# Kept one-hot stores and loads moved from the SyncE queue to the ScalarE queue

## The chip, the cores and the metric

One core of a Trainium2 chip runs the whole program. Its engines are TensorE (PE in the profile, with PEld for the weight loads that overlap it), VectorE (DVE), ScalarE (ACT), GpSimd (POOL) and SyncE (SP). Each engine runs its own instructions in order and waits for other engines at semaphores. A DMA is an instruction of the engine that issues it; the transfer itself runs on 16 DMA engines. The metric is the device time of one execution in microseconds, lower is better.

## What is computed

A block with three parts, on 16 batches of a 32x512 tensor: a point-cloud graph network (the "xattn" part), a Mamba-style scan layer, and a gated feed-forward layer. The change lies in the first part, and there in the gathering of neighbours:

```python
inds_sorted = _sorted_indices(coords.transpose(0, 2, 1))   # 4 space-filling-curve orders of 512 nodes
inds_list = [_window_inds(s) for s in inds_sorted]         # windows of k = 10 neighbours in each order
...
def _get_graph_features(feats, inds_list, perm, W_lin, b_lin, k=K):
    center = feats[:, :, None, :]
    for inds in inds_list:
        neigh = gather(feats, inds)
        gf = concatenate([broadcast(center), neigh - center], axis=-1)
    ...
    scores = einsum('bihd,bjhd->bhij', qh, qh) / sqrt(headdim)
    attn = softmax(scores, axis=-1)
    out = einsum('bhij,bjhd->bihd', attn, qh)
    fused = out @ W_lin.T + b_lin
...
g1 = _get_graph_features(f0, inds_list, perm1, W_lin1, b_lin1)       # layer 1
h1 = einsum('oc,bnkc->bonk', W_conv1, g1);  feats1 = max_k(lrelu(instance_norm(h1)))
g2 = _get_graph_features(feats1, inds_list, perm2, W_lin2, b_lin2)   # layer 2, the same orders
```

Both layers use the same four orders, so they gather through the same permutations.

## The kernel before

All of the graph part is in `graph_part`, in an order written out by hand (L384 switches the planner off). The 16 batches are four groups of four (NBG = 4), and each group has two layers. The eight pairs of group and layer are run as blocks in the order of L1024: (0,0), (1,0), (0,1), (2,0), (1,1), (3,0), (2,1), (3,1). A block has NGRP = 43 iterations of 12 nodes each, and the main loop (L1070) runs through all 344 of them as a software pipeline. In one iteration it emits, in this order: `expo` of the iteration before (a matmul L868 on PE and an exponential L873 on ACT), `turn` (DVE), `scores` (PE, L844 and L851), `rest` and `reduce` (DVE), perhaps one `rank_step` (PE L540, ACT L541), `greatest` (DVE L860), `mapped` (PE L913, ACT copy L918), `sums` (DVE L880), `steps` (see below), `shares` (DVE L886, POOL L888), perhaps another `rank_step`, `outputs` (PE L941), and `differences` for the iteration six ahead (POOL L809). After every third `differences` four DMAs follow (L819, DX<-DD), which SP issues once POOL is done.

`steps` advances a generator, `prep` (L627), by one or two yields. It prepares the next block: every node's position in each order (`rank`) is turned into one-hot matrices `oh` (DVE L751, two orders to a tile of 128x2x512 bf16, 256 KB), and `place` (L701) sorts the features by matmuls with them into `pp` (PE L705, 12 matmuls for a pair of tiles). ACT copies `pp` to `so` (L712), and SP stores it (L716, dS), loads the centres (L681, crep) and loads the sorted features back in windows' layout (L725, fs).

For groups 1 and 2 (`KEPT`, L623) the one-hots made for layer 0 are kept: `keep_it` (L757) stores each tile in DRAM as soon as DVE has written it. That makes 64 stores, k<-oh, 32 in block (0,0) and 32 in block (0,1). In layer 1 of these groups (`at_hand`) they are loaded again instead of being made: `prep` puts the pair (tile, source) in the list `transfers` (L747), and the end of the loop body (L1104) issues what is in the list, after `differences`. That makes 64 loads, oh<-k, 32 in block (2,0) and 32 in block (3,0). There are four `oh` buffers, two pairs; in the `at_hand` form a pair of tiles is loaded in one step of `prep`, and the pair loaded two pairs before is placed in the step ahead of it, which frees its buffers. For the first eight iterations of such a block `steps` takes two steps in an iteration, and then one (L1059 with PREP = 42).

Every DMA of the kernel is issued by SP, in the order in which the code emits it. SP waits for the semaphores of one DMA before it goes on to the next.

Of the kernel before, what the change touches and what calls it, by code (L numbers as in the profile page):

```python
# [53 lines left out]
def kernel(ctx: ExitStack, tc: tile.TileContext, I, out):  # L54
# [65 lines left out]
    with ExitStack() as cx:  # L120
        graph_part(nc, tc, cx, I, dram, id32, ones, xt, U, layernorm_steps, rstd_steps, scan_input)
# [256 lines left out]
def graph_part(nc, tc, cx, I, dram, id32, ones, xt, F0, layernorm_steps, rstd_steps, scan_input):  # L378
# [83 lines left out]
    for t, reps, f in (  # L462
# [4 lines left out]
            out=t4, in_=t4, compare_op=ALU.not_equal, fill=f, base=0,  # L467
            pattern=[[0, reps], [-1, NB], [0, K]], channel_multiplier=1,
        )
    for t, n, f in ((mL.rearrange("p i q -> p (i q)"), P, 1.0), (mR, NI * QB, -BIG)):  # L470
        nc.gpsimd.affine_select(
            out=t, in_=t, compare_op=ALU.not_equal, fill=f, base=-NB,
# [74 lines left out]
    def ranks_of(b):  # L547

        return FIRST // 2 + HALF * (b + 1) if b < 4 else 4 * M * (b + 1)

    def rank_step(tile_of):

        n = ranked[0]
        if n == 4 * M * B:
            return
        ranked[0] += 1
        if n < FIRST:
            half, k = divmod(n, HALF)
            b, c, m = half % 4, k // 2, 2 * (half // 4) + k % 2
        else:  # L560
            b, k = divmod(n, 4 * M)
            c, m = divmod(k, M)
        if n == 0:
            load_keys(0, (0, 1))
        compare(tile_of(n), b, c, m)
        if n < FIRST:
            if k == 1 and half != 3 and half < 7:
                load_keys((half + 1) % 4, (0, 1) if half < 3 else (2, 3))
        elif k == 4 and b + 1 < B:
            load_keys(b + 1, range(M))  # L570
# [54 lines left out]
    transfers = []  # L625

    def prep(g, layer, early=False):  # L627
# [61 lines left out]
        def tick():  # L689
            for t in list(later):  # L690
                t[0] -= 1
                if t[0] <= 0:
                    later.remove(t)
                    t[1]()
# [6 lines left out]
        def place():  # L701
            b, c, ohs, pp = pend.pop(0)
            for m in range(M):
                for k in range(3):
                    nc.tensor.matmul(  # L705
                        pp[32 * m:32 * m + 32, :], lhsT=F3[k][:, c, 32 * b:32 * b + 32], rhs=ohs[m // 2][:, m % 2],
                        start=(c == 0 and k == 0), stop=(c == 3 and k == 2),
                    )
            if c < 3:
                return  # L710
            so = wk.tile([P, D], F32, tag="so", name=f"so{key}_{b}", bufs=2)
            nc.scalar.copy(so, pp)  # L712
            dS = dram.tile([P, D], F32, name=f"dS{key}_{b}")

            def store():
                nc.sync.dma_start(out=dS, in_=so)  # L716

                if not early:
                    centre(b)
                later.append([3, spread])  # L720

            def spread():
                for m in range(M):
                    r = 32 * b + 8 * m
                    nc.sync.dma_start(  # L725
                        out=fs[r:r + 8, :, :D], in_=dS[32 * m:32 * m + 32].rearrange("(h c) n -> c h n", h=4)
                    )

            later.append([2, store])

        for b in range(4):
            while ranked[0] < ranks_of(4 * g + b):
                yield False
            pp = None
            for c in range(4):
                if c == 0:
                    pp = ps_1.tile([P, D], F32, tag="pp", name=f"pp{key}_{b}")
                if at_hand and len(pend) == 2:
                    place()
                    tick()  # L740
                    yield
                ohs = [
                    wk.tile([P, 2, D], BF16, tag="oh", name=f"oh{key}_{b}_{c}_{i}", bufs=4) for i in range(2)
                ]
                for i, oh in enumerate(ohs):
                    if at_hand:
                        transfers.append((oh, kept[g, b, c, i]))  # L747
                        continue
                    for j in range(2):
                        m = 2 * i + j  # L750
                        nc.vector.tensor_scalar(  # L751
                            oh[:, j], it2, rank[:, c, m, 4 * g + b:4 * g + b + 1], None, ALU.is_equal
                        )
                    if layer == 0 and g in KEPT:
                        kept[g, b, c, i] = dram.tile([P, 2, D], BF16, name=f"k{key}_{b}_{c}_{i}")

                        def keep_it(to=kept[g, b, c, i], oh=oh):  # L757
                            nc.sync.dma_start(out=to, in_=oh)

                        later.append([1, keep_it])  # L760
                    if i == 0:
                        tick()
                        yield
                if pend and not at_hand:
                    place()
                pend.append((b, c, ohs, pp))
                tick()
                yield
# [56 lines left out]
    def begin(at):  # L825
        g, layer = order[at]
        L, co, npair, WA, WC, HB = layers[layer]
        key = keys[at]
        per = 4 // npair
        nst = -(-NGRP // per)  # L830
        mxo = wk.tile([P, npair, D], F32, tag="mxo", name=f"mxo{key}")
        stats = wk.tile([P, npair, nst, 6], F32, tag="stats", name=f"stats{key}")
        state[at] = key, co, npair, WA, made[key][2], per, mxo, stats
# [172 lines left out]
    def junk(q):  # L1006
        return wk.tile([P, D], F32, tag="h3", name=f"usq{q}", bufs=1)
# [35 lines left out]
    def steps(at, gi):  # L1043


        if tails:
            if next(tails[0], tails) is tails:
                tails.pop(0)
            if at + 1 >= len(order) or not at_hand(at + 1):
                return  # L1050
        if at + 1 >= len(order):
            return
        if at + 1 not in ahead:
            if at > 0 and gi < 4 and not at_hand(at + 1):
                return
            g, layer = order[at + 1]
            ahead[at + 1] = [prep(g, layer), PREP[layer + at_hand(at + 1)]]
        a = ahead[at + 1]
        for _ in range(2 if a[1] > NGRP - LEAD - SPARE - gi else 1):  # L1059
            if next(a[0], None) is False:  # L1060
                break
            a[1] -= 1

    def wanted(at):

        return ranks_of(4 * min(NBG, 1 + sum(layer == 0 for _, layer in order[:at + 1])) - 1)
# [3 lines left out]
    for it in range(len(blocks) + 5):  # L1070

        def do(step, lag):
            if 0 <= it - lag < len(blocks):
                step(*blocks[it - lag])

        at, gi = blocks[it] if it < len(blocks) else (len(order), 0)
        if gi == 0 and it < len(blocks):
            begin(at)
        do(expo, 1)
        do(turn, 3)  # L1080
        do(scores, 0)
        do(rest, 5)
        do(reduce, 4)
        if ranked[0] < wanted(at):
            rank_step(later_tile)
        do(greatest, 0)
        do(mapped, 0)
        do(sums, 1)
        if at + 1 == len(order) and gi == 4:
            tails.extend(scan_input(sm, junk(q), q) for q in range(NBG - 1))  # L1090
        steps(at, gi)
        do(shares, 1)
        if ranked[0] < wanted(at) and (at == 0 or gi % 2):
            rank_step(later_tile)
        do(outputs, 3)
        if at == 0 and gi < 8:
            rank_step(later_tile)
        if it + LEAD < len(blocks):
            to, g2 = blocks[it + LEAD]
            if g2 == 0:  # L1100
                for _ in ahead[to][0]:
                    pass
            differences(to, g2)
        for oh, of in transfers:  # L1104
            nc.sync.dma_start(out=oh, in_=of)
        transfers.clear()
    for t in (*tails, scan_input(sm, junk(NBG - 1), NBG - 1)):
        for _ in t:
            pass
# [381 lines left out]
```

## Time and profile before

| | |
|---|---|
| time before, median of 3 runs | 2413.45 us (2412.68 to 2421.74) |
| profiled execution, its own time | 2415.22 us |
| its span, first to last instruction | 2413.5 us |
| PE busy over the span | 2189.1 us, 91% |
| DVE, ACT, POOL busy | 1659.9, 1095.5, 831.8 us |
| graph part | to about 1360 us; scan and feed-forward after it |
| stores k<-oh | 64, issued from 132.0 to 520.1 us |
| loads oh<-k | 64, issued from 581.6 to 1003.9 us |
| duration of one such DMA on SP, min / median / max | 319 / 377 / 2276 ns (stores), 319 / 384 / 1921 ns (loads) |

The profile gives busy time of each engine, idle time with the event that ended it, and the order of instructions on each engine. "SPq" rows are DMA instructions on SP's queue; their duration is the issue, not the transfer. A row such as "PE pp L705 <- DMA oh<-k" means that PE's matmul at L705 stood idle until that transfer had landed. The median and the profiled execution differ by 1.8 us, less than a tenth of a per cent.

### The profile page before, as it was taken

What the parts mean: (1) busy time and instruction counts of PE and PEld (TensorE: products, weight loads), DVE (VectorE), ACT (ScalarE), POOL (GpSimd) and SP (SyncE); (2) the same over time, 40 slices, a digit from 0 to 9 for tenths busy, and PEclk for the clock granted to TensorE, in tenths of its full rate; (3) what the DMA queues carried; (4) which work ended last, traced back from release to release, by engine and by line L of the source; (5) the groups of instructions that cost most, each with busy time, mean ns of one, the idle gap of its engine ahead of it and who ended that gap; (6) DMA issues with size and microseconds to landing.
All of it is one profiled execution on the core that took longest, in us unless ns stands there. A gap on an engine that the chain in (4) does not pass through costs nothing. (4 is left out here: it accounts for less than half of the span.)

```text
span 2413.5 us, 88966 instructions
## 1 busy us (share of the span) xinstructions
PE 2189.1 (91%) x39234; PEld 1251.7 (52%) x39234; DVE 1659.9 (69%) x3546; ACT 1095.5 (45%) x2023; POOL 831.8 (34%) x897
## 2 busy tenths in 40 slices
PE   5698899998889997789999789999999999999979
PEld 2254555775446774467777544444444444444422
DVE  8486897987568986689899866554553625446643
ACT  6675576545565553355555322333332424333331
POOL 2154656555455554565555300020210202021200
PEclk9899999999999998999999899999999999999989
DMA  1345232352541325522211312213112131210000
GB/s 48 80 127 144 47 83 57 109 159 76 133 94 44 75 58 130 127 48 65 63 40 40 91 52 78 75 32 91 53 53 71 35 92 46 73 55 20 27 36 18
DMA packets 140058, 171.57 MB, mean 71 GB/s; under 512 B 20446, under 2 KB 81554, under 8 KB 139586
## 3 DMA queue, kind: packets, MB, share of 16 engines
q1 hardware_dynamic: 139672, 165.88, 26.1%
q8 instruction: 308, 5.05, 0.9%
q14 instruction: 78, 0.64, 0.1%
HBM read 93.79 MB, written 29.62 MB: 51 GB/s over the span
## 5 line engine op out<-in xcount | busy, mean ns | idle before, releaser
L888 POOL TENSOR_TENSOR EN<-e,rz 128x480 f32<-128x480 f32 x344 | 342.7, 996 | 564.7 <-DVE rz L886 447.6
L913 PE MATMUL u<-WA,DD 128*32 128x128 bf16 (+1 forms) x16512 | 414.6, 248 | 19.2 <-issue 18.7
L918 ACT COPY us<-u 128x512 f32<-128x512 f32 x516 | 302.3, 587 | 161.0 <-PE u L913 145.5
L913 PEld LDWEIGHTS <-DD 128*32 128x32 f16 x16512 | 338.8, 98 | 53.7 <-issue 51.0
L873 ACT ACTIVATE e<-s,smc 128x480 f32<-128x480 f32 x344 | 227.8, 662 | 286.1 <-PE s L868 258.7
L809 POOL TENSOR_TENSOR DD<-fs,crep 128x480 f16<-128x480 f32 (+2 forms) x344 | 349.8, 1018 | 0.0
L860 DVE TENSOR_REDUCE c<-s 128x16 bf16<-128x480 f32 x344 | 221.3, 643 | 153.3 <-PE s L851 149.7
L941 PEld LDWEIGHTS h<-e,us 128*32 128x32 f32 (+1 forms) x11008 | 251.5, 126 | 133.4 <-issue 70.9
L941 PE MATMUL h<-e,us 128*32 128x30 f32 (+1 forms) x11008 | 285.0, 211 | 27.6 <-issue 12.5
L1189 DVE SCALAR_TENSOR_TENSOR cyh<-ppch,t_conv_w,cyh 128x496 f32<-128x496 f32 (+2 forms) x192 | 137.4, 716 | 221.5 <-ACT cyh L1184 217.5
L1265 POOL TENSOR_TENSOR da<-lei,dA 128x512 f32<-128x512 f32 x32 | 40.6, 1270 | 611.5 <-PE pl L1270 577.4
L1338 PE MATMUL po<-wo,gs 128*128 128x512 f32 x512 | 240.5, 605 | 10.4 <-DVE xt L1341 10.3
L1177 PE MATMUL ppch<-hT,winch 128*128 128x512 f32 x512 | 232.2, 593 | 0.0
L1177 PE MATMUL ppg<-hT,wing 128*128 128x512 f32 x512 | 231.9, 593 | 0.0
L894 DVE STREAM_TRANSPOSE e<-EN 128x512 f32<-128x512 f32 x344 | 224.5, 653 | 0.0
L880 DVE TENSOR_REDUCE z<-e 128x16 f32<-128x480 f32 x344 | 219.9, 639 | 0.1
L541 ACT ACTIVATE sgn<-kd 128x512 bf16<-128x512 f32 x256 | 153.1, 598 | 64.9 <-PE kd L540 61.6
L851 PEld LDWEIGHTS <-DD 128*32 128x32 f16 x5504 | 81.3, 96 | 167.3 <-issue 141.3
L851 PE MATMUL s<-DX,DD 128*32 128x120 f16 x5504 | 142.5, 222 | 25.9 <-DMA DX<-DD 20.2
L1177 PEld LDWEIGHTS ppch<-hT,winch 128*128 128x128 f32 x512 | 93.7, 190 | 122.7 <-issue 122.3
L705 PE MATMUL pp<-oh,F 128*32 128x512 bf16 x1536 | 123.0, 394 | 36.0 <-DMA oh<-k 31.4
L1177 PEld LDWEIGHTS ppg<-hT,wing 128*128 128x128 f32 x512 | 95.8, 190 | 114.1 <-issue 114.0
(327 smaller groups left out, 2851.8 us busy)
## 6 DMA issues: line engine op xcount, KB each, us to landing
DX<-DD SPq DMA_DIRECT2D x456, 90.0 KB
k<-oh SPq DMA_DIRECT2D x64, 256.0 KB
oh<-k SPq DMA_DIRECT2D x64, 256.0 KB
wo<-in_out_proj SPq DMA_DIRECT2D x64, 256.0 KB
wing<-in_in_proj SPq DMA_DIRECT2D x64, 256.0 KB
winch<-in_in_proj SPq DMA_DIRECT2D x64, 256.0 KB
crep<-dC SPq DMA_DIRECT2D x128, 64.0 KB
dS<-so SPq DMA_DIRECT2D x32, 256.0 KB
```

What stands on the lines that cost most here:

```text
L809: nc.gpsimd.tensor_tensor(d[:, :, m0 - n0:n1 - n0], win, crep[:, :, m0:n1].unsqueeze(3).to_broadcast([P, 4, n1 - m0, K]), ALU.subtract,)
L851: nc.tensor.matmul(s[rh, j * 4 * QB:(j + 1) * 4 * QB].rearrange("p (b q) -> p b q", b=4), lhsT=d[:, h, c0:c0 + 32], rhs=dx[:, h, :, c0:c0 ...
L860: nc.vector.tensor_reduce(c, live["s", at, gi].rearrange("p (i q) -> p i q", q=QB), AX.X, ALU.max, negate=True)
L873: nc.scalar.activation(e, s.rearrange("p (i q) -> p i q", q=QB), AF.Exp, scale=smc)
L880: nc.vector.tensor_reduce(z, e, AX.X, ALU.add)
L888: nc.gpsimd.tensor_tensor(en[:, :, :QB], e, rz.unsqueeze(2).to_broadcast([P, NI, QB]), ALU.mult)
L894: nc.vector.transpose(e.rearrange("p i q -> p (i q)"), en.rearrange("p i q -> p (i q)"))
L913: nc.tensor.matmul(u[rh, jj], lhsT=d[:, h, c0:c0 + 32], rhs=WA[k][:, h].rearrange("p b o -> p (b o)"), start=(jj == 0 and k == 0), stop=(k ...
L918: nc.scalar.copy(us[:, j - jj:j + 1], u)
L941: nc.tensor.matmul(h[r:r + co, pr, q0:q0 + QB], lhsT=us[:, j, b * co:(b + 1) * co], rhs=e[:, 4 * j + b, :QB], start=npair > 1, stop=True, ...
L1177: nc.tensor.matmul(pp, lhsT=w[:, k], rhs=hT[:, k], start=(k == 0), stop=(k == 3))
L1338: nc.tensor.matmul(po, lhsT=gs[:, i, q * P:(q + 1) * P], rhs=wo[i], start=(i == 0), stop=(i == TG - 1))
```

## The change

The store in `keep_it` is issued by ACT. The issue of the listed loads moves from the end of the loop body to a point behind `expo`, and ACT issues them. What is put in the list in one iteration is so issued in the next, behind that iteration's exponential. All other DMAs stay with SP.

```diff
                         def keep_it(to=kept[g, b, c, i], oh=oh):
-                            nc.sync.dma_start(out=to, in_=oh)
+                            nc.scalar.dma_start(out=to, in_=oh)
 
                         later.append([1, keep_it])
...
         do(expo, 1)
+        for oh, of in transfers:
+            nc.scalar.dma_start(out=oh, in_=of)
+        transfers.clear()
         do(turn, 3)
...
             differences(to, g2)
-        for oh, of in transfers:
-            nc.sync.dma_start(out=oh, in_=of)
-        transfers.clear()
```

## The prediction

> **What bounds the kernel now.** I read the totals first, then the costliest groups, then SP's own waits, the busy time by stage, and last the order of events around a late one-hot.
>
> ```profile
> PE 2189.1 (91%) x39234; PEld 1251.7 (52%) x39234; DVE 1659.9 (69%) x3546; ACT 1095.5 (45%) x2023; POOL 831.8 (34%) x897
> ...
> L705 PE MATMUL pp<-oh,F 128*32 128x512 bf16 x1536 | 123.0, 394 | 36.0 <-DMA oh<-k 31.4
> ```
>
> PE is the bound as a whole. The last field of the second row is the lead: PE stands 31.4 us before the placing matmuls because a kept one-hot has not landed. Why it is late, SP's queue shows (total us, times, longest us), here from 581 to 685 us, the first stage of loads:
>
> ```profile
> SPq L819 <- POOL DD L809: 27.6, 6, 8.6
> ```
>
> In the second stage, 903 to 1004 us, the same wait is 33.2 us in 7. SP stands at the DX transfers until POOL has made the differences, and whatever was emitted later waits behind it. In order of time (start, duration):
>
> ```profile
> 577.90 0.10 PEld L705 LDWEIGHTS <-F 128*32 128x32 bf16 x1
> ...
> 579.03 2.52 SPq L819 DMA_DIRECT2D DX<-DD  x4
> ...
> 581.60 2.02 SPq L1105 DMA_DIRECT2D oh<-k  x4
> ...
> 584.59 2.19 PE L705 MATMUL pp<-oh,F 128*32 128x512 bf16 x12 [6.46 <-DMA oh<-k]
> ```
>
> PE is ready to place at 577.9. SP waits for POOL until 579.03, issues four DX for 2.5 us, and only then the loads; they land 3.0 us later. The 12 matmuls then take 2.19 us, where twelve with their data at hand take 0.82 us (at 157.16 us). The other stalls over 2 us are 3.99, 3.68, 3.14, 4.44, 5.91 and 2.09 us. Busy time by stage, two of stores and two of loads:
>
> ```profile
> core 0: us, PE busy (x) PEld busy (x) DVE busy (x) ACT busy (x) POOL busy (x), PEclk, DMA share, GB/s
> 132.00:235.00 103.00, 92.86 (x3083) 52.19 (x3081) 82.33 (x192) 68.71 (x158) 57.45 (x58) 0.97 0.51 148
> 453.00:521.00 68.00, 65.63 (x1812) 47.96 (x1812) 62.43 (x164) 32.56 (x54) 33.82 (x34) 1.00 0.64 190
> 581.00:685.00 104.00, 87.88 (x2588) 48.45 (x2588) 63.23 (x136) 56.49 (x130) 47.55 (x48) 0.92 0.51 132
> 903.00:1004.00 101.00, 77.06 (x2519) 49.00 (x2520) 65.55 (x142) 32.75 (x57) 48.22 (x49) 0.88 0.54 136
> ```
>
> In the load stages PE is idle 16.1 and 23.9 us at a clock of 0.92 and 0.88, and no other engine is near full: time won there is kept. In the second store stage PE and DVE are both full: nothing to win there, and something to lose.
>
> **The change, part by part.** *Loads past SP's queue.* 64 loads leave SP, whose place is behind DX, and go to ACT behind the exponential. That exponential needs the matmul L868, which stands on PE behind the placing of the iteration before, so the buffer is free and ACT waits for nothing. With one step an iteration, a pair is then issued over two iterations (about 6 us) ahead of its use. In the first eight iterations of the block there are two steps, and a pair has one iteration. The first pair has none: the exponential ahead of it is that of the very iteration that places it (576.59 to 577.25 us, place at 577.9).
>
> How long does a load need? From the issue of a pair to its first matmul it was 2.9 us (601.78 to 604.70) with little beside it and 6.0 us (631.33 to 637.33) beside DX and crep. With 2.9, the first pair of each stage is still 577.25 + 2.9 - 577.9 = 2.3 us late and no other: 2 x 2.3 = 5 us remain. With 6.0 it is 5.4 us late, and the pairs of the burst, with about 3.7 us to hand, another 2.3 us each for two or three pairs: 2 x (5.4 + 6) = 23 us remain. I take 10, nearer the first, since these loads no longer follow a DX that was itself held back: 31.4 - 10 = 21.4 us won, between 8 and 31.4.
>
> *Slow restart.* Behind four of the stalls the placing took 2.19 and 2.39 us for 12 matmuls, 1.99 for 8 and 1.75 for 10, against 0.82, 0.82, 0.55 and 0.68 at full rate: 5.5 us too long together. Two thirds go with the stalls: 3.7 us, between 0 and 5.5.
>
> *Issue of loads on ACT.* 64 x 0.384 us (SP's median) = 25 us of ACT's time, behind the exponential, ahead of the sign copy and `us`. ACT is busy 56.5 of 104 us in the first stage and 32.8 of 101 in the second, which covers it. In the burst of the first stage an iteration has 0.66 (exponential) + 1.5 x 0.8 (signs) + 0.6 (`us`) + 0.8 (two loads) = 3.3 us of ACT against 3.1 to 3.3 us an iteration: 2 us lost. If SP's longest issue (1.92 us) were the rule in that burst of 12 loads, 12 x 1.5 = 18 us.
>
> *Stores on ACT.* This adds a wait: ACT stands until DVE has written the one-hot, with the next signs and the next exponential queued behind it, and DVE's `sums` and POOL's shares wait for that exponential. Two iterations show the room (first the stage with ranks, then the one without):
>
> ```profile
> 157.38 0.59 ACT L918 COPY us<-u 128x512 f32<-128x512 f32 x1
> 157.41 1.13 DVE L751 TENSOR_SCALAR oh<-it,rank 128x512 bf16<-128x512 f16 x4
> ...
> 158.40 0.60 ACT L541 ACTIVATE sgn<-kd 128x512 bf16<-128x512 f32 x1 [0.43 <-PE kd L540]
> ...
> 159.09 0.66 ACT L873 ACTIVATE e<-s,smc 128x480 f32<-128x480 f32 x1
> ```
>
> ```profile
> 467.40 1.13 DVE L751 TENSOR_SCALAR oh<-it,rank 128x512 bf16<-128x512 f16 x4
> ...
> 470.72 0.64 DVE L880 TENSOR_REDUCE z<-e 128x16 f32<-128x480 f32 x1
> ```
>
> In the first, stores can go at 158.0 and 158.5; with 0.38 us each the sign comes at 158.9 instead of 158.4 and the exponential about 0.6 us late, ahead of `sums` at 160.16 nearly in time. ACT's cycle of 2.85 us (0.66 + 2 x 0.8 + 0.6) becomes 3.6, against 3.55 us an iteration (103 us, 29 exponentials). The block's first iterations, with three signs, have no room at all. I take 5 us for this stage. In the second, the stores end at 468.5 + 0.8 = 469.3, and the exponential (0.66) is done at 470.0, before `sums` at 470.72: hidden by DVE's own 2.2 us of turn, reduce and greatest. Where an issue takes longer (SP needed 6.61 us for six from 458.59), 1.1 us each, the exponential ends at 471.4, 0.7 late: 2 us for the 16 iterations. Together 7 us, between 0 and 35 (with 1.1 us each: the first stage's cycle is 5.05 against 3.55 us, 16 x 1.5 = 24, the second 16 x 0.7 = 11).
>
> *SP without these.* 128 issues leave SP, which in the first store stage stood 31 us at L758 (14.7 + 7.1 + 5.1 + 3.4 + smaller). DX behind them comes earlier: PE waited 2.81 us (at 175.2) and 2.85 us (at 209.1) for it. The first DX was ready at 169.64 by POOL and issued at 170.92, behind a store that took 1.54 us. I take 3 us won, between 0 and 5.7. What remains on SP keeps its order.
>
> One page speaks against the change. The row first: before the late pair, SP's issues of loads were 2.02 us for four, while the wait for POOL ahead of them was up to 8.6 us. The Trainium skill, "DMA: Bandwidth & Descriptors", section "Issuing engines are not separate DMA queues", says that all issuers share the same 16 DMA engines and that spreading the issue saves only the issuing sequencer's own time. Taken as the whole of it, the loads would be no faster and the gain nothing, so that the time would be about 2422, the median and the 9 us of ACT's costs. The row says that the loads lose not transfer time but their place behind another's wait, which that rule leaves out.
>
> **The sum.** -21.4 - 3.7 - 3 + 2 + 7 = -19.1 us. From the profiled 2415.2 that is 2396; from the median, 1.8 us lower, 2394.
>
> **Rivals.** *The loads stay late.* They land after 6 us as at 637, 23 us of stalls remain and the restarts with them: -8 - 1 - 2 + 9 = -2, 2411. For it: the DMA share is already 0.51 to 0.54 there, and a shorter stage moves the same bytes faster. Against it: the second store stage ran at 190 GB/s and share 0.64 with PE full.
>
> *ACT's stores take the place (the slower side).* Each store holds ACT about 1.1 us as from 458.59, because both queues' issues get in each other's way or the ring is full. Then 35 us are lost in the store stages, 10 us in the burst, and the loads win only 21 of their 25: +35 + 10 - 21 = +24, 2437. It decides from the point where a store and its share of the loads cost more than about 0.8 us each. For it: ACT runs nearly back to back around 130 to 170 us. Against it: the median issue is 0.38 us, and ACT is idle half of the second store stage.
>
> **How the numbers follow.** Forecast 0.66, loads stay late 0.15, stores on ACT 0.19. A difference of 0.5%, 12 us, is about what can be told from no change. The forecast's own range is 2376 (stalls 31 + restarts 5.5 + DX 5.7 won, 5 lost) to 2406. The range for 8 in 10 is 2374 to 2424: it takes in the late loads and the milder half of the slower case. Faster by over 0.5% needs under 2401.4: the forecast but for its upper end, 0.62; within 0.5%, that end and the late loads, 0.19; slower 0.19.
>
> **What would show it.** Right: the wait of L705 for oh<-k falls from 31.4 to some 10 us, one stall of 2 to 3 us at each load stage's start; those two stages shorten by about 12 us each and their clock rises above 0.92; SP's waits for DVE oh are gone. Right on the cost: the first store stage grows by under 6 us and the second by under 3. Wrong: long DMA rows on ACT, new waits of DVE's `sums` or of POOL's shares for the exponential, or loads landing over 4 us after their issue. The prediction fails most easily on the price of one store on ACT.

## The result and the profile after

The changed kernel takes 2411.27 us (median of 20 runs, 2401.80 to 2434.74) against 2414.67 us for the kernel before (median of 20 runs, 2404.97 to 2421.74). The ratio of the means is 0.9999, with a 95% interval of 0.9982 to 1.0016 (the medians lie 3.4 us apart): no difference that can be measured, where 19 us were forecast. The profiled execution spans 2416.9 us, against 2413.5 before.

First the totals and the group of matmuls that now leads in waiting (engine busy time; then one group's busy time, mean ns, and the idle time ahead of it with its main cause):

```profile
PE 2191.0 (91%) x39234; PEld 1254.1 (52%) x39234; DVE 1660.5 (69%) x3546; ACT 1088.4 (45%) x2023; POOL 831.6 (34%) x897
...
L851 PE MATMUL s<-DX,DD 128*32 128x120 f16 x5504 | 143.7, 224 | 43.6 <-DMA DX<-DD 39.3
```

The amount of work has not changed. What PE waits for has. From the waits of the changed kernel (engine, line, what it waited for: us in all, times, longest):

```profile
PE s L851 <- DMA DX<-DD: 39.3, 8, 14.7
...
PE pp L705 <- DMA oh<-k: 6.5, 5, 2.5
```

and the row of the kernel before that answers to the first of them:

```profile
PE s L851 <- DMA DX<-DD: 20.2, 3, 14.5
```

The wait for kept one-hots fell by 24.9 us, to 6.5, as the change was meant to do. In its place the score matmuls stand 19.1 us longer for DX, a transfer that the change does not touch and that is still issued by SP. One wait of some 14.5 us at the start is common to both. Why DX is late shows in SP's own waits, which the prediction did not expect to grow. In the changed kernel:

```profile
SPq L819 <- DMA oh<-k: 25.0, 9, 7.8
SPq L681 <- DMA k<-oh: 16.4, 5, 7.0
...
SPq L819 <- DMA k<-oh: 12.7, 9, 3.1
...
SPq L725 <- DMA oh<-k: 11.7, 6, 5.2
```

SP, which no longer issues a kept one-hot, now waits for them to land: before DX (L819), the centres (L681) and the sorted features (L725), which neither read nor write a one-hot. Before the change the longest entry of this kind was 3.0 us in all:

```profile
SPq L535 <- DMA oh<-k: 3.0, 3, 2.1
```

The reason lies in the semaphores. The trace tells which semaphore each transfer counts on. All DMAs of SP and ACT together use eight of them, numbered 101 to 108, in turn: each of the eight is used about 171 times, and in the changed kernel each has 152 to 162 transfers of SP and 9 to 19 of ACT. A transfer starts only when the one that had its semaphore before it has landed, whichever engine issued that one: in the trace the instruction that issues it carries a wait for the very semaphore that it will count on (SP's at 627.67 us below waits for 107 and counts on 107). While SP issued everything, the transfer eight places back had nearly always landed: SP's waits for such transfers were 10.7 us in all. With two issuers the turns are no longer taken in the order of time. The first load stage shows it, on ACT (start, duration, what; idle time and its cause in brackets):

```profile
623.85 0.58 ACT L1014 COPY h<-p 128x512 f32<-128x512 f32 x1 [3.03 <-PE p L1012]
...
624.90 0.33 ACTq L1081 DMA_DIRECT2D oh<-k  x1
624.91 0.66 ACT L873 ACTIVATE e<-s,smc 128x480 f32<-128x480 f32 x1
625.32 0.40 ACTq L1081 DMA_DIRECT2D oh<-k  x1
```

and on SP's queue over the same time:

```profile
621.17 12.74 SPq L819 DMA_DIRECT2D DX<-DD  x6
```

ACT stood 3 us for a matmul of another part of the program, so its loads started at 624.90 and 625.32. Two of SP's DX transfers had their turn behind these very loads. Worked out from the trace's semaphore events (start, landing, semaphore, and what had the semaphore before):

```
SP  DX  621.17 -> 623.43  106
ACT oh  624.90 -> 627.65  107
ACT oh  625.32 -> 630.29  101
SP  DX  627.67            107   after ACT's oh, landed 627.65
SP  DX  628.30            108
SP  DX  630.30            101   after ACT's oh, landed 630.29
```

Both times SP starts 0.01 to 0.02 us after ACT's load has landed. A group of four DX that took 2.5 us before takes from 621.2 to about 630.9 here (SP's row holds two more, of the next group). Added up by this rule over the graph part, from 130 us on, SP waits 100.4 us for transfers of ACT and 26.3 us for its own, where it was those 10.7 us for its own before. That SP is idle costs nothing; DX late for PE does. Lines of the two blocks that hold the loads, by their start and end in each kernel, first before, then after (window, its length, busy time of each engine, granted clock of PE, DMA share, GB/s):

```profile
569.20:741.20 172.00, 145.92 (x4504) 82.12 (x4503) 112.94 (x237) 100.14 (x226) 87.75 (x97) 0.94 0.42 105
897.10:1057.60 160.50, 124.27 (x4441) 80.22 (x4440) 112.53 (x237) 59.62 (x101) 87.36 (x97) 0.93 0.44 108
```

```profile
580.90:744.30 163.40, 141.52 (x4508) 80.89 (x4507) 113.28 (x237) 98.38 (x227) 87.31 (x97) 0.96 0.44 110
903.50:1058.70 155.20, 123.32 (x4441) 79.24 (x4440) 112.79 (x237) 59.24 (x100) 87.31 (x97) 0.95 0.44 113
```

These blocks became 8.6 and 5.3 us shorter, at a higher clock. But the first of them begins 11.7 us later, at 580.9 instead of 569.2: the three blocks ahead of it, which hold the stores, took that much more. The gain and the loss, each shown again below by itself, cancel. (The rest of the program, in which nothing was edited, was 5.6 us longer in this one profile.)

### The profile page after: what moved, and what is told of

Its sections match the earlier page's. It is cut to its first block, busy times and chain, and to the rows that moved or that the text cites. A ratio compares the mean times of both kernels' runs of the same rounds, so it can differ in the third digit from the quotient of the medians.

```text
span 2416.9 us, 88938 instructions
## 1 busy us (share of the span) xinstructions
PE 2191.0 (91%) x39234; PEld 1254.1 (52%) x39234; DVE 1660.5 (69%) x3546; ACT 1088.4 (45%) x2023; POOL 831.6 (34%) x897
## 5 line engine op out<-in xcount | busy, mean ns | idle before, releaser
L913 PE MATMUL u<-WA,DD 128*32 128x128 bf16 (+1 forms) x16512 | 421.8, 251 | 27.1 <-issue 26.9
L913 PEld LDWEIGHTS <-DD 128*32 128x32 f16 x16512 | 343.6, 99 | 66.0 <-issue 62.3
L1338 PE MATMUL po<-wo,gs 128*128 128x512 f32 x512 | 240.5, 605 | 10.4 <-DVE xt L1341 10.3
L851 PEld LDWEIGHTS <-DD 128*32 128x32 f16 x5504 | 82.5, 97 | 188.1 <-issue 157.2
L1338 PEld LDWEIGHTS po<-wo,gs 128*128 128x128 f32 x512 | 90.6, 190 | 108.1 <-issue 90.2
```

Source lines behind the costliest of these rows:

```text
L851: nc.tensor.matmul(s[rh, j * 4 * QB:(j + 1) * 4 * QB].rearrange("p (b q) -> p b q", b=4), lhsT=d[:, h, c0:c0 + 32], rhs=dx[:, h, :, c0:c0 ...
L913: nc.tensor.matmul(u[rh, jj], lhsT=d[:, h, c0:c0 + 32], rhs=WA[k][:, h].rearrange("p b o -> p (b o)"), start=(jj == 0 and k == 0), stop=(k ...
L1338: nc.tensor.matmul(po, lhsT=gs[:, i, q * P:(q + 1) * P], rhs=wo[i], start=(i == 0), stop=(i == TG - 1))
```

## The experiments

Three theories were set against each other. **L**: the shared turn of the semaphores is the price; transfers on ACT hold up SP's. **A**: the price is ACT's own time and its waits, ahead of the exponential. **B**: it is the bytes, which get in each other's way wherever they are issued. Each ratio below is against runs of the kernel before on the same chip, with its 95% interval. "SP for ACT" is SP's waiting for transfers of ACT, worked out as above.

**The two parts alone.** Loads on ACT behind the exponential, stores still on SP:

```diff
+        for oh, of in transfers:
+            nc.scalar.dma_start(out=oh, in_=of)
+        transfers.clear()
         do(turn, 3)
...
-        for oh, of in transfers:
-            nc.sync.dma_start(out=oh, in_=of)
-        transfers.clear()
```

> Only the 64 loads are issued by ACT behind the exponential; the stores stay on SP. Theory L (completion semaphores: all transfers of SP and ACT share eight of them in turn, so an SP transfer also waits for the landing of the ACT transfer that had its semaphore before): the two load stages look as in the changed kernel, with L705's wait for oh<-k near 6.5 us instead of 31.4, SP waiting some 50 us for oh<-k in the load stages, and DX stalls of about 12 us there; the store stages look as in the kernel before. Time 8 to 14 us under the kernel before, about 2402. Theory A (the price of the change lies in ACT's stores alone, in its waits for DVE and the late exponentials): the same time, 2400 to 2405, but no gain given back in the load stages: DX stalls there under 3 us. Theory B (both queues' bytes share the 16 DMA engines, so whatever the loads win the DX transfers lose): no faster than before, DX landing in over 3.5 us at the median in the load stages.

Measured: 0.9949 (0.9933 to 0.9966), 2398.24 us against 2409.41. From its waits:

```profile
PE s L851 <- DMA DX<-DD: 31.3, 7, 14.7
...
PE pp L705 <- DMA oh<-k: 6.7, 5, 2.0
```

24.7 us of the wait for one-hots are gone and 11.1 us of waits for DX have come: 13.6 us are left, and the time fell by 11.2. SP for ACT is 52.7 us, all of it in the two blocks that hold the loads (27.4 and 25.3). There PE stands 7.0 and 6.1 us for DX: L had expected about 12 us together and A under 3.

Stores on ACT, loads still on SP:

```diff
                         def keep_it(to=kept[g, b, c, i], oh=oh):
-                            nc.sync.dma_start(out=to, in_=oh)
+                            nc.scalar.dma_start(out=to, in_=oh)
```

> Only the 64 stores are issued by ACT; the loads stay on SP at the end of the loop body. Theory L: SP waits about 45 to 50 us for k<-oh in the two store stages, against under 2 before; time 6 to 12 us over the kernel before, about 2423. Theory A: the same time, but with DVE's sums waiting over 5 us for the exponential and few waits of SP for k<-oh. Theory B: within 4 us of the kernel before. L705's wait for oh<-k stays at 25 to 35 us in all of them.

Measured: 1.0039 (1.0022 to 1.0057), 2419.41 us against 2409.41. The waits of PE, and below them one of SP's:

```profile
PE pp L705 <- DMA oh<-k: 30.9, 12, 6.4
PE s L851 <- DMA DX<-DD: 30.6, 5, 15.1
```

```profile
SPq L681 <- DMA k<-oh: 14.3, 5, 6.5
```

The wait for DX is 10.4 us longer, and the time 10.0 us. SP for ACT is 42.4 us, where L had 45 to 50 and A little; DVE's wait of `sums` for the exponential is 4.7 us, where A had over 5. B, which expected less than 4 us of loss, is off. So the change is the sum of a part that wins about 0.5% and one that loses about 0.4%. A store has no reader for hundreds of microseconds, yet SP's load of the centres waits for stores to land.

**Place or queue.** If the loads' place behind DX was the trouble, they can be moved ahead of DX and stay on SP:

```diff
+        for oh, of in transfers:
+            nc.sync.dma_start(out=oh, in_=of)
+        transfers.clear()
         if it + LEAD < len(blocks):
             to, g2 = blocks[it + LEAD]
...
             differences(to, g2)
-        for oh, of in transfers:
-            nc.sync.dma_start(out=oh, in_=of)
-        transfers.clear()
```

> Everything stays on SP; the loads are emitted one place earlier, ahead of differences and its DX instead of behind them. If it is enough to pass the DX of the same iteration: L705's wait for oh<-k falls to 10 to 18 us, DX stalls in the load stages stay near 0, time 2398 to 2406. If the loads are held by the DX of an earlier iteration: the wait stays at 25 to 31 us and the time within 5 us of the kernel before. Theory L adds that no wait of SP for oh<-k over 10 us appears, since with one queue the transfer that had the semaphore before was issued earlier anyway.

Measured: 0.9928 (0.9911 to 0.9946), 2393.44 us against 2409.41. SP waits 11.7 us for its own transfers and for none of ACT:

```profile
PE s L851 <- DMA DX<-DD: 18.9, 3, 14.7
...
PE pp L705 <- DMA oh<-k: 18.4, 13, 3.4
```

The wait for one-hots falls by less than on ACT, since SP may still stand at something else, but none of DX's comes in its place. The same lines with ACT as the issuer (the edit above with `nc.scalar.dma_start`), stores on SP:

> As e3_loads_sp_first, with the loads emitted ahead of differences, but issued by ACT: only the queue differs. Theory L: SP waits some 50 us for ACT's loads again, DX stalls of 8 to 14 us in the load stages, ratio 0.994 to 0.998. If the place in the program alone made e3_loads_sp_first better than e1_loads_act: ratio 0.991 to 0.994 and DX stalls near 0 there.

Measured: 0.9893 (0.9868 to 0.9919), 2388.72 us against 2414.11.

```profile
PE s L851 <- DMA DX<-DD: 27.0, 5, 14.9
...
PE pp L705 <- DMA oh<-k: 1.0, 1, 1.0
```

Better than both expectations; L had 0.994 to 0.998. SP for ACT is 43.4 us, so the turn costs here too, 6.8 us of DX's wait, but the loads, issued in the same iteration in which they are listed and not in the next, are late but once. The change moved the loads to a new queue and at the same time to a later place, behind the next iteration's exponential; in that place (the first experiment) 6.7 us of the wait remain, in this one 1.0. So with ACT as the issuer the place makes 0.9949 into 0.9893, clear of the intervals; at the same place ACT's queue makes SP's 0.9928 into 0.9893, with intervals that just overlap.

**Turn or bytes.** With the pair of tiles made one tile, a pair is one DMA of 512 KB, in the changed kernel: the same bytes in half as many turns.

```diff
+                both = wk.tile([P, 4, D], BF16, tag="oh", name=f"oh{key}_{b}_{c}", bufs=2)
+                ohs = [both[:, 2 * i:2 * i + 2] for i in range(2)]
...
+                        if i == 0:
+                            transfers.append((both, kept[g, b, c]))
```

> The changed kernel with the two tiles of a pair made one tile of 512 KB, so that 32 stores and 32 loads of 512 KB are issued by ACT in place of 64 and 64 of 256 KB; a store then waits for all four one-hots of a pair. Theory L: half as many semaphores are held by ACT's transfers, SP's waits for them fall from 100 us to some 50, the DX stalls (24 us beside the one at the start) to about 14; 5 to 10 us under the changed kernel. Theory A: stores fall to half, ACT loses less, 2 to 5 us under. Theory B: the same bytes, no change.

Measured: 0.9989 (0.9975 to 1.0002), 2405.93 us against 2409.41. SP for ACT is 87.5 us where L had expected about half of 100: a miss. The waits are fewer, 25 against 51, but longer, 3.5 us each against 2.0: a load of 512 KB landed after 4.5 us at the median, one of 256 KB after 3.7. The run does not tell the theories apart.

The opposite: the loads on ACT, and behind each a transfer of 64 bytes whose result nobody reads, so that there are more turns and no more bytes to speak of.

```diff
         for oh, of in transfers:
             nc.scalar.dma_start(out=oh, in_=of)
+            idle = dram.tile([1, 16], F32, name=f"idle{len(idles)}")
+            nc.scalar.dma_start(out=idle, in_=ones[0:1, 0:16])
+            idles.append(idle)
         transfers.clear()
```

> Loads on ACT and stores on SP as in e1_loads_act, and behind every load ACT issues a second transfer of 64 bytes to a DRAM tile of its own that nobody reads: 64 small transfers on top, so that ACT's transfers hold twice as many of the shared completion semaphores. Theory L: SP's waits for ACT's transfers rise from 53 us to 80 to 100, DX stalls beside the one at the start from 16.6 to 22 us or more, and the ratio to the kernel before from 0.995 to 0.997 to 1.000. Theory A (ACT's time counts): 64 issues of 0.33 us are 21 us of ACT's time, mostly under cover: ratio within 0.001 of 0.995, DX stalls unchanged. Theory B (bytes): no change, 4 KB in all.

Measured: 0.9986 (0.9966 to 1.0005), 2410.89 us against 2413.08. Nearly all of the 0.5% that the loads on ACT win is gone, as L has it. In the profile SP for ACT rose only from 52.7 to 57.0 us, less than L expected, and PE's waits for DX beside the one at the start were 15.3 us, where L had 22 or more, though that execution (2399.01 us) is the fastest of its twelve. The time fits L, the profile hardly does. These 64 transfers are also new ones, and further below such transfers on ACT cost time while SP waits little for them, so that this run does not show that the turn is the price.

POOL's transfers do not take part in the turn: they have semaphores of their own (111 to 118). The loads of the first experiment with `nc.gpsimd.dma_start`:

> Loads issued by POOL at the place where the changed kernel has them, stores on SP. POOL's transfers have a semaphore row of their own, so theory L has no coupling here: SP's waits for oh<-k fall under 5 us, the DX stalls of the load stages under 4 us, and the ratio is 0.990 to 0.995 if POOL's issue costs it little. If POOL's issue is dear (over 1 us each, 64 us of POOL in two stages where it is half busy), the differences come late and the ratio is 0.996 to 1.003 with POOL waits taking the place. Theory B: DX stalls of some 12 us stay in the load stages, since the bytes and their time are the same.

Measured: 0.9959 (0.9941 to 0.9977), 2402.73 us against 2413.08. The same place, the same bytes, and the waits for DX are what they were before the change:

```profile
PE s L851 <- DMA DX<-DD: 20.2, 3, 14.9
...
PE pp L705 <- DMA oh<-k: 15.7, 7, 4.6
```

SP waits for no load here, 11.6 us for its own transfers. The one-hots are later than from ACT; POOL has its own work ahead of them and 0.54 us for each issue, and they land 4.3 us after it at the median, against 3.7 from ACT. PE's two waits add up to 35.9 us, with ACT to 38.0, and the times of the two kernels cannot be told apart (0.9959 and 0.9949). The same for the stores alone, on POOL:

> Stores issued by POOL where ACT issued them, loads on SP as before. Neither ACT's time nor the semaphores shared by SP and ACT are touched. Theories L and A: SP's waits for k<-oh are gone and the first block is no slower than before; ratio 0.996 to 1.001. Theory B, or a dear issue on POOL: 1.003 or more, which the first block's iterations would show.

Measured: 0.9988 (0.9971 to 1.0004), 2411.23 us against 2413.08, PE's wait for DX 16.2 us. On ACT the same bytes cost 0.4%, on POOL nothing that was measured: B falls. The Trainium skill, "DMA: Bandwidth & Descriptors", section "Issuing engines are not separate DMA queues", has all issuers end on the same DMA engines, which leaves the issuer's own time as the only difference. By time of issue POOL is the dearer one, 0.58 us a store against ACT's 0.33; the runs show the cheaper issue losing, so the rule is not the whole of it here.

**ACT's time and waits.** The stores on ACT, but held back for two steps of the generator and not one, meant to spare ACT the wait until DVE has written the one-hot (in the second experiment, `later.append([2, keep_it])`):

> Stores on ACT as in e2_stores_act, but each is issued one step of the preparation later, when DVE has had time to write the one-hot; loads on SP as before. Theory A (ACT stands at a store until DVE is done, with signs and exponentials behind it): the loss falls from 0.4% to under 0.2%, and the waits of DVE's sums for the exponential from 4.7 us to under 2. Theory L: SP's waits for k<-oh stay over 35 us and the ratio stays at 1.003 to 1.005.

Measured: 1.0030 (1.0009 to 1.0050), 2420.35 us against 2413.08: no better than without the delay within the intervals. DVE's wait of `sums` for the exponential is 3.0 us, where it is 4.7 without the delay, and SP's waits for the stores have stayed (SP for ACT 41.5 us):

```profile
SPq L681 <- DMA k<-oh: 15.8, 6, 5.4
```

But the delay does not do what it was meant to. Around 460 to 485 us two stores together hold ACT for 1.5 to 2.3 us, as here:

```profile
461.61 2.26 ACTq L758 DMA_DIRECT2D k<-oh  x2
```

Each of the two issues is 0.33 us. Between them ACT stands until 463.5, when DVE has written the one-hot of the second store: these iterations take two steps, so that one of the two stores still waits for a one-hot of the same iteration. In all ACT stands 20.3 us for DVE at its stores here, against 14.2 without the delay, and the run does not speak against A. A cleaner test leaves the stores with SP and gives ACT an operation that waits for the same one-hot and takes the time of an issue:

```diff
                             nc.sync.dma_start(out=to, in_=oh)
+                            nc.scalar.copy(sgn[:, :160], oh[:, 1, :160])
```

> The kernel before, with all transfers on SP, and on ACT at each of the 64 stores a copy of 128x160 bf16 out of the one-hot just written, about 0.33 us, into scratch: ACT has the wait for DVE and the time of a store's issue, but no transfer. Theory A (ACT's wait and time are the price of the stores): ratio 1.002 to 1.005, and the first eight iterations over 31 us as with the stores on ACT, against 28.6. Theory L: ratio within 0.0015 of 1, the first eight iterations near 28.6 us, SP's waits for k<-oh under 3 us.

Measured: 0.9997 (0.9980 to 1.0013), 2414.02 us against 2414.11. The rows of the copy and of ACT's wait ahead of it:

```profile
L759 ACT COPY sgn<-oh x64: 321/325/328, 130.2 to 507.8; 128x160 bf16<-128x160 bf16 x64
```

```profile
ACT sgn L759 <- DVE oh L751: 38.0, 54, 2.8
```

ACT stands 38 us at the place where the store was and works 64 x 0.325 = 21 us there (the stores in the second experiment took 27.6 us), and the program is not slower: A, as it was put, falls. The block's first eight iterations do take 31.0 us instead of 28.6, as with the stores on ACT, but that is made up later.

The last test gives ACT a DMA at the same place that carries 32 bytes, the stores staying on SP:

```diff
                             nc.sync.dma_start(out=to, in_=oh)
+                            few = dram.tile([1, 16], BF16, name=f"few{len(fews)}")
+                            nc.scalar.dma_start(out=few, in_=oh[0:1, 1, 0:16])
```

> The kernel before with all its transfers on SP, and at each of the 64 stores a transfer of 32 bytes out of the one-hot, issued by ACT into a DRAM tile that nobody reads. Beside e10_act_time, where ACT had the same wait and about the same 0.33 us but no transfer (0.9997), only the shared completion semaphores differ; the bytes are 2 KB in all. Theory L: SP waits 25 us or more for these small transfers, and the ratio is 1.002 to 1.005, as with the stores themselves on ACT (1.0039). If the semaphores aren't the cause: SP waits under 8 us for them, ratio within 0.0015 of 0.9997.

Measured: 1.0052 (1.0033 to 1.0071), 2425.22 us against 2410.96. So 64 more transfers of next to no bytes, issued by ACT, cost 0.5%, as much as moving the stores there, while an operation of 0.325 us with the same wait costs nothing; the issue of one of them takes 0.20 us. The loss needs neither the bytes nor that much of ACT's time, then. The same small transfers from another engine were not run, so that their number alone is not ruled out. And SP waits for these transfers only 11.8 us in all, less than half of what L expected, and for its own 21.2, and PE's waits for DX and one-hots are nearly as before (21.9 and 29.6 us). The largest new row in the second store stage, at ACT's exponential (L877 here), does not tell the two tests apart. Waits from 440 to 560 us, and one of them in order of time:

```profile
ACT e L877 <- DVE rz L890: 36.5, 15, 4.4
```

```profile
467.74 0.73 ACTq L761 DMA_DIRECT2D few<-oh  x2
468.56 0.66 ACT L877 ACTIVATE e<-s,smc 128x480 f32<-128x480 f32 x1 [2.09 <-DVE rz L890]
```

The 2.09 us of idle time run up to 468.56 and so take in the two small transfers and what ACT waited for ahead of them, DVE's one-hot; `rz` is only the DVE instruction that ended nearest by. With the copy in their place the same wait stands under the copy's name, over the same window:

```profile
ACT sgn L759 <- DVE oh L751: 27.0, 31, 2.2
```

The loss is spread: in the three blocks up to the first loads PE was idle 47.2 us, against 37.2 before and 33.4 with the copy, and only 6.8 us of it were for DX (5.7 before). The last 27 iterations of the third block, by the starts of their exponentials, took 106.0 us; in the kernels that leave single stores to SP or POOL they took 97.0 to 103.7 (100.1 before), and 100.8 with the stores themselves on ACT. How much of the loss goes through SP and how much through ACT is therefore not settled for this kernel, and by the same token not for the stores.

**Versions that beat both.** Loads ahead of DX on SP and stores on POOL, so that no DMA is on ACT:

> e3_loads_sp_first with the stores issued by POOL as in e8_stores_pool. If the two gains add (0.9928 and 0.9988): ratio about 0.9916, 2393 us; if the store stages have nothing to give: 0.993.

Measured: 0.9892 (0.9860 to 0.9925), 2388.06 us against 2414.11. Loads ahead of DX on ACT and stores on POOL:

> e13_act_ahead with the stores issued by POOL as in e8_stores_pool. If the gains add (0.9893, 0.9988): 0.988, some 2385 us; if the one uses what the other frees: 0.989 to 0.991.

Measured: 0.9902 (0.9879 to 0.9926), 2387.83 us against 2410.96. Loads ahead of DX on SP with pairs as one DMA:

> e3_loads_sp_first with the pair's tiles as one tile and one transfer of 512 KB, all on SP: 32 stores and 32 loads in place of 64 and 64. Theory L has little to say with one queue. If the number of issues on SP counts (64 fewer, 0.4 to 0.6 us each, part of it ahead of DX): ratio 0.990 to 0.992. If the longer single transfer makes its first half late: 0.993 to 0.996.

Measured: 0.9986 (0.9971 to 1.0001), 2409.63 us against 2414.11, a miss: the gain of the place is lost again. A pair's buffer is free only when all 512 KB have been stored, and DVE waits for that (the kernel before has 7.1 us in this row's place). By the table below 15.4 us are lost up to the first loads, where this row lies, and 10.0 in the blocks with loads, which it does not explain:

```profile
DVE oh L751 <- DMA k<-oh: 18.1, 9, 5.1
```

The first two of these and the loads ahead on ACT with stores on SP (0.9893) cannot be told apart by their intervals, so that moving the stores to POOL adds nothing that was measured once the loads are on ACT and early.

**All profiles side by side.** Each span cut in three: up to the start of the first block with loads (it holds the stores), the two blocks with loads, and the rest, in which nothing was edited; beside it PE's waits for one-hots and for DX. All from one profiled execution each, in us.

```
                                stores   loads    rest   oh<-k    DX
before                           569.2   332.5  1511.8    31.4  20.2
stores on POOL                   560.3   329.3  1520.7    30.8  16.2
copy on ACT                      561.6   329.9  1512.9    27.9  15.3
loads on ACT                     564.8   313.7  1518.0     6.7  31.3
loads on ACT, doubled            560.9   318.4  1518.1     6.5  30.0
loads on POOL                    567.7   315.7  1515.4    15.7  20.2
loads ahead, SP                  567.0   304.5  1516.6    18.4  18.9
loads ahead, ACT                 565.1   309.9  1518.5     1.0  27.0
loads ahead, SP; stores POOL     562.4   308.2  1523.5    12.7  15.8
loads ahead, ACT; stores POOL    562.6   303.3  1516.2     4.3  18.5
loads ahead, SP; pairs           582.4   314.5  1517.3    18.1  14.6
stores on ACT                    574.9   323.4  1519.4    30.9  30.6
stores on ACT, later             573.7   331.8  1515.5    29.3  24.3
32 bytes on ACT                  582.2   325.2  1517.7    29.6  21.9
the change                       580.9   318.6  1517.4     6.5  39.3
the change, pairs                579.7   308.1  1515.9     5.0  37.2
```

The first column falls into two groups: 560.3 to 569.2 where ACT issues no DMA in the stores' stages and the stores are single, 573.7 to 582.4 else. The second does too: 323.4 to 332.5 where the loads stand behind DX on SP, 303.3 to 318.6 else. The third, without any edit, spreads over 11.7 us, which is how much a single profile can mislead. One more figure goes with the stores: in the first block the granted clock of PE was 0.913 to 0.947 in the four kernels whose stores ACT issues, and 0.954 to 0.985 in all others. Whether the stalls there bring the clock down was not tested.

## Why the prediction was wrong

The step that failed is "SP without these": "DX behind them comes earlier", with 3 us won, and "What remains on SP keeps its order". SP does issue in its old order, but the step took its transfers for independent of those that had left. In truth DX's waits grew by 19.1 us, since DX, the centres and the sorted features share eight semaphores in turn with what ACT issues. The single parts have 11.1 us more of them with the loads moved and 10.4 with the stores. As a term of the sum: -3 was forecast, +19 is what the profile after shows. With +19 in its place the sum is +3 us, and the runs put the change between 4 us faster and 4 us slower.

*Loads past SP's queue.* Right, and close: 10 us of stall were to remain, 6.5 did. The landing time was sized well too: median 3.7 us, one in ten over 5.4 (2.9 to 6.0 had been taken).

*Slow restart.* Right in its direction and larger: the placing matmuls (L705) were busy 123.0 us before, 116.7 after and 117.0 with the loads alone on ACT, so 6 us less where 3.7 were forecast, with an upper bound of 5.5. The blocks with loads ran at a clock of 0.96 and 0.95 instead of 0.94 and 0.93, which is the direction forecast.

*Issue of loads on ACT.* 64 issues took 30.4 us of ACT in all, against 25 in the estimate. No run isolates a cost of it.

*Stores on ACT.* 7 us were taken, with bounds of 0 and 35; the part alone costs about 9 to 10 us. The size is near, the reason was another. It was costed as ACT's time in front of the exponential, and ACT given that wait and most of that time without a DMA loses nothing. PE's wait for DX, not listed in this step at all, rose by what the part lost. What the 32-byte transfers show leaves open that ACT has a share. The bound of 35 rested on a wrong reading: the 6.61 us for six stores from 458.59 are not 1.1 us an issue. The six issues add up to 2.95 us, 0.49 us each, and the rest is SP's wait for DVE between them.

*The rivals.* "The loads stay late" gave 2411, the time that was measured, but by a mechanism that did not occur: the loads are in time. "ACT's stores take the place" rightly saw that the stores lose what the loads win, but put the point of decision at 0.8 us a store; they took 0.46 us on average, and the loss came all the same, by another way. A third rival was missing: transfers that stay behind wait for those that left. The line of the kernel before from which it could have been asked was there, SP's 3.0 us at L535 for a one-hot that L535 has nothing to do with.

*What would show it.* The load stages were to be shorter by about 12 us each; the blocks that hold them became 8.6 and 5.3 shorter. The second store stage was to grow by under 3 us and the first by under 6; up to the first load block it was 11.7. One of the signs of being wrong did appear: DVE's `sums` wait 7.1 us in all for the exponential, and the kernel before has no such row.

## What to carry to other kernels

Before moving a DMA to another queue, ask first whether its place in the old one can be moved: with the loads on SP, a few lines further up won 0.7%, where the move to ACT's queue won 0.5% (the intervals overlap) and brought new waits. The better place counts on ACT's queue too: there it won 1.1%, in spite of the waits. In a trace, look for an issuer that waits for a transfer whose data its own DMA has no use for; that is a shared resource of the queues, here the semaphore turn, and the waits for it grow when the issuers no longer run in step. And measure the parts of a change singly: the two of this one were worth -0.5% and +0.4%, and together they looked like nothing.

## What the hardware and the runs showed that was not expected

A transfer on ACT's queue can hold up SP's without sharing data with it: SP's next transfer started 0.01 to 0.02 us after ACT's had landed. Whether another assignment of semaphores would remove this was not tried. Transfers issued by POOL stand apart from this turn, at 0.54 to 0.58 us an issue, against 0.33 us (median) for a 256 KB store on ACT and 0.20 us for one of 32 bytes. The median of a load's landing was 3.84 us from SP, 3.68 from ACT and 4.29 from POOL.

Left open: why 64 transfers of 32 bytes on ACT cost as much as 64 of 256 KB, when SP waits for them so much less; and whether loads ahead of DX gain from ACT's queue at all, since 0.9893 there and 0.9928 on SP are not clear of each other.
